# An adaLN transformer block in f32 on one core: the work of the last two batches placed anew, and the last sums turned by TensorE in two parts

## The chip, the cores and the metric

The kernel runs on one core of a Trainium2 chip. Its engines are TensorE (PE, with its weight loads shown as PEld), VectorE (DVE), ScalarE (ACT), GpSimd (POOL) and SyncE (SP), which here issues nearly all transfers. The metric is the time of one execution on the device in microseconds, lower is better; three runs stand beside one profiled execution.

## The reference

Eight batches of 1024 tokens with 256 features, all in f32. A modulation of six vectors per batch (shift, scale and gate, twice) comes from a small product. Then:

```
h = layernorm(x) * (1 + ca) + sa
q, k, v = split(h @ w_in.T)                     # 16 heads of 16
attn = softmax(causal(q k^T / 4)) v
x = x + ga * (attn @ w_out.T + b_out)
h = layernorm(x) * (1 + cb) + sb
prev = h shifted by one token, zero ahead of the first
xr = mu_r * h + (1 - mu_r) * prev ;  xk = mu_k * h + (1 - mu_k) * prev
x = x + gb * sigmoid(xr @ W_r.T) * (relu(xk @ W_k.T)^2 @ W_v.T)
```

The second half needs each token's neighbour, so the second chunk of a batch needs one column ("edge") of the first.

## The kernel before

**Tiling.** A batch b is cut into chunks c of 512 tokens (x is c = 0, y is c = 1 in the tables below). Heads go in groups of four; a unit u = 4b + g is one group of one batch, 32 units in all. Each head sits in a strip of 32 partitions. The scores of a unit are computed twice: `maxima` (S) makes them with the queries on partitions (`pp`), in two banks at a time from the pool `ps_s` (2 buffers of two banks), and DVE takes the largest of each row, adding a causal mask on diagonal blocks; `subtract` turns the maxima (`pmx`) and writes their negative into a spare row of q (`q<-mrow`, a transfer). `weights` (T) makes the scores again with the keys on partitions (`pw`, one bank per head, four banks from the pool `ps_t`, 4 buffers); ACT takes the exponential out of each bank and POOL clears the masked triangle. `attend` multiplies the weights with v, which has a column of ones, so each head's sum comes out as an extra row (`po`, ACT copies it, POOL adds the later parts). The pieces of a unit are the steps a to e (diagonal blocks) and 0 to 3 (whole blocks); the last two units (30 and 31) use the parts f, g, h, i so that chunk 0 is done first.

**The order.** One step of the program (`step`, line 977) takes one piece of T, LAG = 9 places behind S, interleaves the products of both, and then places small work: what `soon` holds for this step, the fill of this step from the tables, and `attend` of the piece before. There are 290 pieces, steps 0 to 298; from step 290 on there is no S left ("alone"). The tables POST, PREP and END name, by step relative to a batch's first, when the parts of `post(b, c)` are placed: load, bias, project0/2 (`py`, attention output times w_out, added to x by DVE), stats and norm (DVE and POOL, on ACT in the ordered stretch), turn (`ptb`, transposes by PE, evacuated by ACT), mix (POOL: difference of neighbours), mixed (DVE: four multiply-adds of 128x512), receptance0/2 (`pr`, tanh on ACT), key0/1 (`pk`, relu on ACT, square on POOL), value0/2 (`pkv`, times r on DVE, added to x on POOL, then the output's transfer). POST for batch 6 starts at step 261; END places x of batch 7 there too, and `tail` does y of batch 7 after the last step.

**What fixes the order.** PE's queue is always in the order of the program text. While `strict` is set (all of the steps), DVE, ACT, POOL and SP keep it too, so an instruction that waits holds up all that stands behind it on its engine. In `tail` a scheduler orders the other engines. `later` puts a transfer off to the next step.

**Sums.** For most units the row of sums goes out and comes back through memory: `gather` stores o (`od`), loads oT from it, and every second unit `spread_sums`, `invert`, `write_over`, `read_over` and `divide` follow over seven steps. For chunk 1 of units 30 and 31, `gather_last` (line 686) does it on the chip: four transposes by PE (`psum`), a reciprocal and a broadcast on DVE (`wide`), a product with the identity (`pinv`), a multiply on DVE, then four transfers of 16 partitions from o into oT.

All small products and turns take their bank from `ps_t` through `bank`, the pool that also holds the four banks of `pw`. After the last step the kernel does x's key and value, and then `tail`.

Of the kernel before, what the change touches and what calls it, by code (L numbers as in the profile page):

```python
# [14 lines left out]
P = 128  # L15
# [57 lines left out]
def adaln_block(  # L73
# [23 lines left out]

    def bank(name):
        return ps_t.tile([P, CW], F32, tag="t", name=name)

    issued = {}
    strict = [False]
# [533 lines left out]
    def groups_of(u):  # L636
        return GROUPS_APART if u >= B * NG - 2 else GROUPS
# [32 lines left out]
    def gather(u, c):  # L670
# [12 lines left out]
            lambda: sync.dma_start(S["oT"][at : at + HG * HD, g // 2, :], od[:, :HD, :])  # L683
        )

    def gather_last(u, c):

        o = U[u]["o", c]
        b, g = divmod(u, NG)
        pt = bank(f"psum{u}")  # L690
        for t in range(NT):
            pe.transpose(pt[:, t * P : (t + 1) * P], o[:, t * P : (t + 1) * P], ident)
        inv = sb.tile([P, NT, HG], F32, tag="few", bufs=2, name=f"inv{u}")
        dve.reciprocal(inv, pt.rearrange("p (t j s) -> p t j s", t=NT, s=ST)[:, :, :, HD])
        wide = sb.tile([P, NT, HG, ST], F32, tag="over", bufs=2, name=f"wide{u}")
        dve.tensor_copy(wide, inv.unsqueeze(3).to_broadcast([P, NT, HG, ST]))
        po = bank(f"pinv{u}")
# [9 lines left out]
        for j in range(HG):  # L707
            at = (g % 2) * HG * HD + j * HD
            queue = act if j % 2 and u == B * NG - 1 else sync
            queue.dma_start(  # L710
                A[b, c]["oT"][at : at + HD, g // 2, :], o[j * ST : j * ST + HD, :]
            )

    def spread_sums(b, c, d):

# [29 lines left out]
    def post(b, c):  # L745
# [12 lines left out]
            return S["x"][:, t0 : t0 + 2, :].rearrange("p t e -> p (t e)")  # L758

        def project(t0):  # L760
            py = bank(f"py{b}_{c}_{t0}")
            rows(py, S["oT"], G[b]["wo"], (t0, t0 + 1))
            dve.tensor_add(flat(t0), flat(t0), py)

# [36 lines left out]
            )  # L801

        def receptance(t0):
            pr = bank(f"pr{b}_{c}_{t0}")
            rows(pr, S["mix"], wr_sb, (t0, t0 + 1))
            r = sb.tile([P, CW], F32, tag="r", bufs=2, name=f"r{b}_{c}_{t0}")
            act.activation(r, pr, AF.Tanh, scale=0.5)
            S["r", t0] = r

        def key(e):  # L810
            pk = bank(f"pk{b}_{c}_{e}")
# [12 lines left out]
            pool.tensor_mul(ka, ka, ka)  # L824

        def value(t0):
            pv = bank(f"pkv{b}_{c}_{t0}")
            rows(pv, S["ka"], G[b]["wv"], (t0, t0 + 1))
            r = S["r", t0]

            dve.scalar_tensor_tensor(r, r, 1.0, pv, ALU.add, ALU.mult)
            pool.tensor_add(flat(t0), flat(t0), r)
            if t0:
                later(lambda: sync.dma_start(tokens(out, b, c), S["x"]))

        def tail():

            def both(f):  # L840
                f(0)
                f(1)
# [2 lines left out]
                return slice(half * CW // 2, (half + 1) * CW // 2)  # L845

            both(lambda half: project(2 * half))
            st = sb.tile([P, NT, 6], F32, tag="st", bufs=2, name="st_last")
            mv = sb.tile([P, NT, 2], F32, tag="mv", bufs=2, name="mv_last")
            rs = sb.tile([P, NT], F32, tag="rs", bufs=2, name="rs_last")  # L850
# [2 lines left out]
            def normal(half):  # L853
                ts = (2 * half, 2 * half + 1)
                for t in ts:
                    dve.bn_stats(st[:, t, :], S["x"][:, t, :])
                    dve.bn_aggr(mv[:, t, :], st[:, t, :])
                of = slice(2 * half, 2 * half + 2)
                dve.tensor_scalar_add(rs[:, of], mv[:, of, 1], EPS)
                pool.tensor_tensor(rs[:, of], rs[:, of], m_half[:, of], ALU.pow)  # L860
                for t in ts:
                    dve.tensor_scalar(
                        h[:, t, :],
                        S["x"][:, t, :],
                        mv[:, t, 0:1],
                        rs[:, t : t + 1],
                        ALU.subtract,
                        ALU.mult,
                    )

            both(normal)
            h2T = sb.tile([P, DC, CW + 1], F32, tag="h2T", name="h2T_last")
            pool.tensor_copy(h2T[:, :, 0:1], A[b, 0]["edge"])
# [95 lines left out]
            value0=lambda: value(0),  # L969
            value2=lambda: value(2),  # L970
            tail=tail,
        )

# [38 lines left out]
    def finish(T, now):  # L1012
# [240 lines left out]
```

## Time and profile before

| | us |
|---|---|
| median of three runs (1415.96 to 1418.1) | 1417.32 |
| the profiled execution, own time | 1422.07 |
| its span, first to last instruction | 1420.3 |
| PE busy | 1392.3 |
| DVE, ACT, POOL busy | 1062.8, 894.0, 553.3 |
| step 290 (first without S), start of its `pw_h` | 1325.2 |
| last `po_i` ends | 1380.5 |
| first `py` of the tail | 1394.05 |
| last product ends | 1415.6 |

The page gives busy times over the span, then the span in 40 slices as tenths, and then groups. In a line of the timeline stand the start, the time, the engine, the line of the program, the operation, out<-in with their shapes, how many instructions were merged, and in brackets the idle time before it with what ended it. In a line of stretches stand the stretch, its length, busy time and number of instructions of PE, PEld, DVE, ACT and POOL, then the granted clock of PE as a share, the DMA share and GB/s. All small operations carry the line of one helper (L115), so they are told apart by the names of their tiles. A name that ends in `_last` belongs to the tail.

### The profile page before, as it was taken

What the parts mean: (1) busy time and instruction counts of PE and PEld (TensorE: products, weight loads), DVE (VectorE), ACT (ScalarE), POOL (GpSimd) and SP (SyncE); (2) the same over time, 40 slices, a digit from 0 to 9 for tenths busy, and PEclk for the clock granted to TensorE, in tenths of its full rate; (3) what the DMA queues carried; (4) which work ended last, traced back from release to release, by engine and by line L of the source; (5) the groups of instructions that cost most, each with busy time, mean ns of one, the idle gap of its engine ahead of it and who ended that gap; (6) DMA issues with size and microseconds to landing.
All of it is one profiled execution on the core that took longest, in us unless ns stands there. A gap on an engine that the chain in (4) does not pass through costs nothing.

```text
span 1420.3 us, 29753 instructions
## 1 busy us (share of the span) xinstructions
PE 1392.3 (98%) x11256; PEld 765.3 (54%) x11256; DVE 1062.8 (75%) x2869; ACT 894.0 (63%) x1693; POOL 553.3 (39%) x840
## 2 busy tenths in 40 slices
PE   9999999999999999999999999999999999999997
PEld 5544555555554555555555555545555555455455
DVE  6777787788777777788777887787777887887234
ACT  3466676666676666666666766766666666575441
POOL 1142242445422444425433454324534344244341
PEclk9999999999999999999999999999999999999988
DMA  5512423232222323231232322223231321201111
GB/s 190 183 34 81 128 76 113 62 102 84 91 73 69 107 83 110 68 101 64 83 113 62 106 80 98 66 69 106 84 105 59 106 89 38 83 32 43 41 32 33
DMA packets 81271, 118.96 MB, mean 84 GB/s; under 512 B 10208, under 2 KB 38752, under 8 KB 81128
## 3 DMA queue, kind: packets, MB, share of 16 engines
q1 hardware_dynamic: 80792, 116.74, 25.4%
q8 instruction: 88, 1.44, 0.4%
q14 instruction: 55, 0.45, 0.1%
q10 hardware_dynamic: 336, 0.33, 0.1%
HBM read 71.17 MB, written 45.09 MB: 82 GB/s over the span
## 4 chain that ended last, share of the span: by engine, by line
PE 91%; DMA 3%; DVE 2%; ACT 2%; POOL 1%; issue 1%; SPq 0%; POOLq 0%; ACTq 0%; DVEq 0%
PE pw L115 12%; PE po L115 8%; PE pp L115 7%; PE pq L115 6%; PE po_c L115 5%; PE po_e L115 5%; PE py L115 4%; PE pkv L115 4%; PE pr L115 4%; PE pk L115 4%; PE pv L115 4%; PE pw_a L115 3%; PE pw_e L115 2%; PE pmx L115 2%; PE pw_c L115 2%; PE pp_d L115 2%
## 5 line engine op out<-in xcount | busy, mean ns | idle before, releaser
L115 DVE TENSOR_REDUCE max<-pp 128x2 f32<-128x1024 f32 x256 | 301.9, 1218 | 63.4 <-PE pp L115 61.2
L115 ACT ACTIVATE w<-pw 128x512 f32<-128x512 f32 x512 | 265.2, 602 | 95.3 <-PE pp L115 59.6
L115 PE MATMUL pw<-q,k 32*128 32x512 f32 x1024 | 267.0, 618 | 0.4 <-ACT w_i L115 0.4
L115 PE MATMUL pp<-k,q 32*128 32x512 f32 x1024 | 256.7, 620 | 0.0
L115 PEld LDWEIGHTS pw<-q,k 32*128 32x128 f32 x1024 | 108.7, 184 | 99.8 <-issue 57.4
L115 DVE DVE_READ_ACCUMULATOR2_ANT max<- 128x1 f32 x1024 | 144.8, 141 | 0.0
L115 DVE CUSTOM_DVE_ANT_0 pp_c<-pp_c,mask 128x256 f32<-128x256 f32 x240 | 102.3, 436 | 46.8 <-PE pp_c L115 40.6
L115 DVE CUSTOM_DVE_ANT_0 pp_b<-pp_b,mask 128x128 f32<-128x128 f32 x240 | 102.3, 437 | 43.5 <-PE pp_b L115 37.2
L115 DVE CUSTOM_DVE_ANT_0 pp_e<-pp_e,mask 128x512 f32<-128x512 f32 x128 | 88.3, 707 | 52.5 <-PE pp_e L115 50.3
L115 DVE CUSTOM_DVE_ANT_0 pp_d<-pp_d,mask 128x128 f32<-128x128 f32 x240 | 102.4, 437 | 28.9 <-PE pp_d L115 22.8
L115 PE MATMUL po<-w,v 128*32 128x512 f32 x1024 | 123.1, 598 | 0.0
L115 PE MATMUL pq<-hT,wqk_sb 128*128 128x512 f32 x240 | 114.3, 608 | 1.0 <-ACT hT L115 1.0
L115 POOL TENSOR_TENSOR xb<-xb,r 128x512 f32<-128x512 f32 x30 | 41.4, 1379 | 148.9 <-DVE r L115 123.9
L115 DVE CUSTOM_DVE_ANT_0 pp_a<-pp_a,mask 128x512 f32<-128x512 f32 x128 | 87.8, 707 | 12.9 <-PE pp_a L115 10.8
L115 ACT ACTIVATE w_a<-pw_a 128x512 f32<-128x512 f32 x128 | 66.2, 602 | 41.8 <-PE pp_a L115 40.3
L115 POOL TENSOR_TENSOR rsb<-rsb,m_half 128x2 f32<-128x2 f32 x30 | 21.5, 715 | 177.5 <-DVE rsb L115 177.4
L115 POOL TENSOR_TENSOR o<-o,more 128x512 f32<-128x512 f32 x62 | 79.1, 1276 | 28.2 <-ACT more L115 28.2
L115 PEld LDWEIGHTS pp<-k,q 32*128 32x128 f32 x1024 | 82.7, 183 | 3.9 <-DVE max L115 3.6
L115 ACT ACTIVATE w_d<-pw_d 128x512 f32<-128x512 f32 x120 | 63.1, 601 | 19.9 <-PE pp_e L115 19.6
L115 ACT ACTIVATE w_e<-pw_e 128x512 f32<-128x512 f32 x128 | 66.2, 603 | 14.2 <-PE pp_c L115 13.4
L115 ACT ACTIVATE w_b<-pw_b 128x512 f32<-128x512 f32 x120 | 62.1, 602 | 18.1 <-PE pp L115 17.6
L115 ACT ACTIVATE w_c<-pw_c 128x512 f32<-128x512 f32 x120 | 62.2, 603 | 14.9 <-PE pp_b L115 10.7
(207 smaller groups left out, 3046.4 us busy)
## 6 DMA issues: line engine op xcount, KB each, us to landing
od<-o SPq DMA_DIRECT2D x62, 256.0 KB
pad<-qk SPq DMA_DIRECT2D x60, 256.0 KB
q<-pad SPq DMA_DIRECT2D x30, 512.0 KB
k<-pad SPq DMA_DIRECT2D x30, 512.0 KB
xa<-in_x SPq DMA_DIRECT2D x16, 512.0 KB
xb<-in_x SPq DMA_DIRECT2D x16, 512.0 KB
oT<-od SPq DMA_DIRECT2D x62, 128.0 KB
ov<-over SPq DMA_DIRECT2D x31, 256.0 KB
```

What stands on the lines that cost most here:

```text
L115: made = f(*args, **kwargs)
```

## The change

- A flag `late` is set at the first step without S. From then on `bank_apart` takes the banks of `py`, `pr`, `pk` and `pkv` from the pool of the maxima (`ps_s`).
- `gather_last` is cut in two: `turn_sums` (psum, reciprocal, wide) one step after a unit's end, and the rest (pinv, multiply, transfers) one step later. Units 30 and 31 now do this for chunk 0 too, which went through memory before; its four transfers are put off by a step.
- A table POST_LAST takes the place of POST for batch 6 while batch 7 is attended, and END names earlier steps for x of batch 7.
- A step without S and without fill gets five transposes of the identity (`heat`); this is the case in step 298.
- x's key of batch 7 goes around the last `pinv`; x's value is cut into its product (`multiplied`) and the rest (`valued`), which `tail` places between its own parts. The second half of the tail's normalisation goes from DVE to ACT.

```diff
+    late = [False]
+    def bank_apart(name):
+        if late[0]:
+            return ps_s.tile([P, 2, CW], F32, tag="s", name=name)[:, 0, :]
+        return bank(name)
...
-    def gather_last(u, c):
+    def turn_sums(u, c):
         o = U[u]["o", c]
-        pt = bank(f"psum{u}")
+        pt = bank(f"psum{u}_{c}")
         for t in range(NT):
             pe.transpose(pt[:, t * P : (t + 1) * P], o[:, t * P : (t + 1) * P], ident)
...
+        U[u]["wide", c] = wide
+    def gather_last(u, c):
+        o, wide = U[u]["o", c], U[u]["wide", c]
...
+        def side_by_side():
+            for j in range(HG):
+                at = (g % 2) * HG * HD + j * HD
+                queue = act if j % 2 and c and u == B * NG - 1 else sync
+                queue.dma_start(
+                    A[b, c]["oT"][at : at + HD, g // 2, :], o[j * ST : j * ST + HD, :]
+                )
+        if c:
+            side_by_side()
+        else:
+            later(side_by_side)
...
-        def value(t0):
-            pv = bank(f"pkv{b}_{c}_{t0}")
+        def multiplied(t0):
+            S["pv", t0] = pv = bank_apart(f"pkv{b}_{c}_{t0}")
             rows(pv, S["ka"], G[b]["wv"], (t0, t0 + 1))
-            r = S["r", t0]
+        def valued(t0):
+            r, pv = S["r", t0], S["pv", t0]
...
             both(lambda half: project(2 * half))
+            other["multiplied0"]()
...
+                if half:
+                    pool.tensor_mul(away, mv[:, of, 0], rs[:, of])
+                    pool.tensor_scalar_mul(away, away, -1.0)
+                for n, t in enumerate(ts):
+                    if half:
+                        act.activation(h[:, t, :], S["x"][:, t, :], AF.Identity,
+                            bias=away[:, n : n + 1], scale=rs[:, t : t + 1])
+                        continue
...
-            both(turned)
+            turned(0)
+            other["multiplied2"]()
+            turned(1)
...
             both(mixed_half)
+            other["valued0"](), other["valued2"]()
...
         alone = not (T and S)
+        if not S and not late[0]:
+            late[0] = True
...
+        if not S and not fill:
+            pt = bank_apart(f"heat{now}")
+            for n in range(5):
+                pe.transpose(pt[:, :P], ident, ident)
...
-            if u >= B * NG - 2 and c:
-                soon.append((now + 1, lambda: gather_last(u, c)))
+            if u >= B * NG - 2:
+                soon.append((now + 1, lambda: turn_sums(u, c)))
+                soon.append((now + 2, lambda: gather_last(u, c)))
                 return
...
+    POST_LAST = """
+    -12 x.load; -6 x.bias; 4 x.project0; 6 x.project2; 7 x.stats0; 7 y.load; 8 x.stats1; 8 y.bias;
+    9 x.norm0; 9 y.project0; 10 x.norm1; 10 x.turn; 11 x.mix; 11 y.project2; 12 x.mixed00;
+    12 y.stats0; 13 x.mixed01; 13 x.mixed10; 13 x.receptance0; 14 x.mixed11; 15 x.receptance2;
+    15 y.stats1; 16 y.norm0; 17 x.key0; 17 y.norm1; 18 x.key1; 18 y.turn; 19 y.mix; 20 x.value0;
+    20 y.mixed00; 21 y.mixed01; 21 y.mixed10; 22 x.value2; 22 y.mixed11; 22 y.receptance0;
+    23 y.receptance2; 24 y.key0; 25 y.key1; 26 y.value0; 27 y.value2
+    """
...
     END = """
-    26 x.load; 28 x.bias; 32 x.project0; 32 x.project2; 33 x.stats0; 33 x.stats1; 34 x.norm0;
-    34 x.norm1; 35 x.turn; 35 x.mix; 36 x.mixed00; 36 x.mixed01; 36 x.mixed10; 36 x.mixed11;
-    36 y.load; 37 y.bias; 37 x.receptance0; 37 x.receptance2
+    16 x.load; 18 x.bias; 26 y.load; 28 x.project0; 28 y.bias; 29 x.project2; 30 x.stats0;
+    30 x.stats1; 31 x.norm0; 32 x.norm1; 32 x.turn; 33 x.mix; 34 x.mixed00; 34 x.mixed01;
+    34 x.mixed10; 34 x.mixed11; 35 x.receptance0; 36 x.receptance2
     """
...
-            place(POST, at, x=ready[b - 1][0], y=ready[b - 1][1])
+            place(POST if b < B - 1 else POST_LAST, at, x=ready[b - 1][0], y=ready[b - 1][1])
...
+    for n, f in ((1, "key0"), (2, "key1")):
+        soon.append((len(slots) + n, ready[B - 1][0][f]))
+    soon.sort(key=lambda z: z[0])
...
-    for f in ("key0", "key1", "value0", "value2"):
-        ready[B - 1][0][f]()
-    ready[B - 1][1]["tail"]()
+    ready[B - 1][1]["tail"](ready[B - 1][0])
```

For comparison, the entries of POST that y used before: project0 15, project2 17, turn 20, mix 21, mixed 22 to 25, receptance 28 and 29, key 29 and 31, value 33 and 35.

More of the change, by code (lines that the diff above doesn't have):

```diff
@@ L684, in gather @@
         )
-    def gather_last(u, c):
+    def turn_sums(u, c):
         o = U[u]["o", c]
-        b, g = divmod(u, NG)
-        pt = bank(f"psum{u}")
+        pt = bank(f"psum{u}_{c}")
         for t in range(NT):
             pe.transpose(pt[:, t * P : (t + 1) * P], o[:, t * P : (t + 1) * P], ident)
-        inv = sb.tile([P, NT, HG], F32, tag="few", bufs=2, name=f"inv{u}")
+        inv = sb.tile([P, NT, HG], F32, tag="few", bufs=2, name=f"inv{u}_{c}")
         dve.reciprocal(inv, pt.rearrange("p (t j s) -> p t j s", t=NT, s=ST)[:, :, :, HD])
-        wide = sb.tile([P, NT, HG, ST], F32, tag="over", bufs=2, name=f"wide{u}")
+        wide = sb.tile([P, NT, HG, ST], F32, tag="over", bufs=2, name=f"wide{u}_{c}")
         dve.tensor_copy(wide, inv.unsqueeze(3).to_broadcast([P, NT, HG, ST]))
-        po = bank(f"pinv{u}")
+        U[u]["wide", c] = wide
+    def gather_last(u, c):
+        o, wide = U[u]["o", c], U[u]["wide", c]
+        b, g = divmod(u, NG)
+        po = bank(f"pinv{u}_{c}")
         for t in range(NT):
@@ L706, in gather_last @@
         dve.tensor_mul(o, o, po)
[L707 to L712, printed above, removed]
+        def side_by_side():
[9 more added lines that the diff above has]
+            later(side_by_side)
     def spread_sums(b, c, d):
@@ L760, in project @@
         def project(t0):
-            py = bank(f"py{b}_{c}_{t0}")
+            py = bank_apart(f"py{b}_{c}_{t0}")
             rows(py, S["oT"], G[b]["wo"], (t0, t0 + 1))
@@ L803, in receptance @@
         def receptance(t0):
-            pr = bank(f"pr{b}_{c}_{t0}")
+            pr = bank_apart(f"pr{b}_{c}_{t0}")
             rows(pr, S["mix"], wr_sb, (t0, t0 + 1))
@@ L810, in key @@
         def key(e):
-            pk = bank(f"pk{b}_{c}_{e}")
+            pk = bank_apart(f"pk{b}_{c}_{e}")
             for d in range(DC):
@@ L834, in value, with tail @@
                 later(lambda: sync.dma_start(tokens(out, b, c), S["x"]))
-        def tail():
+        def tail(other):
             def both(f):
@@ L860, in normal @@
                 pool.tensor_tensor(rs[:, of], rs[:, of], m_half[:, of], ALU.pow)
-                for t in ts:
+                if half:
[3 more added lines that the diff above has]
+                    if half:
+                        act.activation(
+                            h[:, t, :],
+                            S["x"][:, t, :],
+                            AF.Identity,
+                            bias=away[:, n : n + 1],
+                            scale=rs[:, t : t + 1],
+                        )
+                        continue
                     dve.tensor_scalar(
@@ L869, in normal @@
                     )
+            away = sb.tile([P, 2], F32, tag="away", bufs=2, name="away_last")
             both(normal)
@@ L968, in post @@
             key1=lambda: key(1),
-            value0=lambda: value(0),
-            value2=lambda: value(2),
+            multiplied0=lambda: multiplied(0),
+            multiplied2=lambda: multiplied(2),
+            valued0=lambda: valued(0),
+            valued2=lambda: valued(2),
+            value0=lambda: (multiplied(0), valued(0)),
+            value2=lambda: (multiplied(2), valued(2)),
             tail=tail,
```

## The prediction

> **What bounds the kernel now.** I read the page's busy shares first, then its slices, then the stretches of the last 130 us by the granted clock, then the timeline of TensorE (PE) with the waits in brackets, and last the other engines around those waits. Over the span PE is the bound, and the clock it was granted sags only in the last two slices:
>
> ```profile
> PE 1392.3 (98%) x11256; PEld 765.3 (54%) x11256; DVE 1062.8 (75%) x2869; ACT 894.0 (63%) x1693; POOL 553.3 (39%) x840
> PEclk9999999999999999999999999999999999999988
> ```
>
> These are stretches of the last 130 us; the third last column is the granted clock, 0.50 in each:
>
> ```profile
> 1335.30:1338.70 3.40, 3.40 (x8) 0.90 (x11) 0.00 (x0) 0.84 (x3) 0.63 (x1) 0.51 0.00 0
> 1362.70:1366.10 3.40, 3.40 (x10) 2.65 (x9) 0.08 (x1) 1.09 (x3) 0.83 (x2) 0.50 0.00 0
> 1372.90:1376.30 3.40, 3.40 (x9) 2.69 (x10) 1.04 (x2) 0.96 (x3) 2.22 (x5) 0.50 0.01 4
> 1400.30:1407.00 6.70, 5.04 (x14) 3.90 (x15) 5.58 (x16) 2.11 (x5) 0.70 (x1) 0.50 0.00 0
> ```
>
> The waits of PE there, and the one of DVE from which the first of them comes:
>
> ```profile
> 1297.01 2.33 DVE L115 SCALAR_TENSOR_TENSOR mix<-step,mus,h2T 128x512 f32<-128x512 f32 x2 [1.19 <-POOL step L115]
> 1300.59 1.07 PE L115 MATMUL pp_i<-k,q 32*128 32x256 f32 x8 [1.75 <-DVE max L115]
> 1362.38 3.53 PE L115 MATMUL pkv<-wvb,ka 128*128 128x256 f32 x8 [1.31 <-ACT w_e L115]
> 1381.33 0.66 PE L115 MATMUL psum<-ident,o 128*128 128x128 f32 x4 [0.87 <-DVE o L115]
> 1382.89 1.81 PE L115 MATMUL pinv<-ident,wide 128*128 128x128 f32 x8 [0.90 <-DVE wide L115]
> 1390.93 3.29 PE L115 MATMUL pkv<-wvb,ka 128*128 128x256 f32 x14 [1.02 <-POOL ka L115]
> 1394.05 3.62 PE L115 MATMUL py<-wob,oT 128*128 128x256 f32 x16
> 1399.33 0.78 PE L115 MATMUL pt_last<-ident,h_last 128*128 128x128 f32 x4 [1.66 <-DVE h_last L115]
> 1401.96 1.14 PE L115 MATMUL pt_last<-ident,h_last 128*128 128x128 f32 x4 [1.85 <-DVE h_last L115]
> 1403.01 3.75 PE L115 MATMUL pr<-wr_sb,mix_last 128*128 128x256 f32 x8
> 1408.53 1.89 PE L115 MATMUL pr<-wr_sb,mix_last 128*128 128x256 f32 x8
> ```
>
> A busy PE is not a fast one: the same `pr` takes 3.75 us at 1403 and 1.89 at 1408. In the last 130 us the clock falls at 1301.2, 1335.3, 1345.6, 1362.7, 1372.9, 1383.1 and 1400.3; all gaps are multiples of 3.41 us, and each fall lasts 3.4 us (the last twice that). So the clock is decided on a grid of 3.41 us, and a stretch costs 1.7 us where PE has work throughout. Ahead of each fall stand either a gap of PE or the 32-row products `pw` without `pp` beside them: 0.44 us of gap was enough at 1372.3.
>
> Prices at full clock: a product of eight 128x256 records (py, pr, pk, pkv) 1.73 us (1408.53 to 1410.25); pw with pp 1.86; pw alone 1.9; po 1.86, po_i 2.36; a final sum's four transposes 0.66; pinv 0.9 (half of the 1.81 at half clock).
>
> **The change part by part.** Steps count from 0; all up to 289 have maxima (S) beside weights (T); steps 290 to 298 have weights alone. In the profile 290 begins at 1325.2, and po_i ends at 1380.5.
>
> *Steps 265 to 289 (batch 6 sooner; chunk 0's last sums on chip).* Six products (one pr, two pk, two pkv of batch 6, one py of batch 7) leave the alone steps for these: 6 x 1.73 = 10.4 us, work that PE does either way, so zero. Added on PE: psum and pinv for two units, 2 x 1.56 = 3.1, 2.8 as their drains overlap (bounds 2.4 and 3.6, at half clock partly). SP loses two stores through memory, their reads, and one chain of inverses; it gains eight issues on oT at 0.62 (2.47 for four). Four of those stand in step 288 ahead of the last batch's out and of `q<-mrow`, which is wanted four steps later; py of step 289 wants them. The multiply is done about 4 us into 287, issues and landing take 2.5 + 2.0 (a store of od at 1308.93, its read at 1310.94), py starts 12 us into it: hidden, with 3.3 us to spare. Without it PE would wait for the remainder.
>
> DVE is the danger here. In steps 280 to 282 the masked maxima stand close: e 3.0, h 2.5 + r 0.69 + mix 0.70, i 3.35 + reciprocal 0.53 + two mixes 1.4 + join 0.1: 12.3 us against PE's 2.3 + 3.35 + 4.2 = 9.9. DVE begins a step 1 us behind PE and PE may run two banks ahead, so I take 1.6 us of gaps (bounds 0, the lead covers it, and 5: the excess plus two waits for POOL like the 1.19 above). Steps 271 to 276 come out even (DVE: maxima 15.3, four mixes 2.8, two statistics 2.5, an addition 0.7, a reciprocal 0.5: 21.8; PE: six times 1.86, ptb 0.9, three products 5.2, pmx 0.4, two po of a first half 4.7: 22.4), so I take 0.4. In return the gap at 1298.8 (1.75), its half clock (1.7) and 0.35 before it go: y's mixes come a step after POOL's subtraction and beside r, not into h. One half stretch after the new gaps, one in two: 0.85. Sum: +3.8 - 2.85 - 2.8 = **-1.85** (loss).
>
> *Steps 290 to 298.* Lost before: gaps 0.44 + 0.29 + 0.96 + 1.31 + 0.44, pw slower for its banks 0.4 (2.27) and 0.7 (pw_e 2.59), four half stretches 6.8: 11.3. Late products now sit in the banks of maxima, so pr no longer queues behind exponentials, and the 0.96 of pinv goes because pw of the next step lies between it and psum. What stays: pw of step 292 after pw_i (0.44 + 0.4), psum behind POOL's addition (0.3), pw_e right behind pw_3 (0.7). What is new: the turn of batch 7's mix (ptb) now stands in 293, ahead of pw_2, behind four exponentials (2.07) and two halves of hb (0.52 each) on ACT; it is ready about 1.85 us after pw_1, psum fills 0.75: 1.1 us (bounds 0 and 1.9), and all later weights queue behind it. That is 2.9. Half clock: less full-width work lies between the pw, so I take three chances of 3/4 at 1.7: 3.8 (bounds 0 and 6.8). Heat, five transposes: 0.5 (bounds 0.4 and 1.1, by the same count at half clock). Sum: 11.3 - 6.7 - 0.5 = **+4.1**.
>
> The Trainium skill ("TensorE: Matmul & The Clock Gate", HAM oscillation) says that only idle gaps of more than about 3.4 us cost the clock. The row of 0.44 us above differs, so the measurement decides; by the rule the half-clock terms of this sum would be zero. The same page (Part 4, PE-mode transpose) says that transposes do not count as activity for the clock; no run here shows it, and it speaks against heat: the 0.5 would buy nothing, and psum with ptb would leave a cold window for certain.
>
> *The tail, from po_i's end (t).* Before: psum at t + 0.87, py at t + 13.6, end at t + 39.8. After, s = t + 0.87: psum to s + 0.45, pk to 2.2, pinv to 3.05 (wide waits inside pk), multiply 3.25 to 3.95. The issues on SP and ACT take 1.15 and 1.42, the second leaves about 0.7 in, landing 2.0: oT at s + 6.7. The second pk ends at 4.8, so PE waits 1.95: a new stall, which was covered by pkv before. py starts at t + 7.6, **6.0 sooner**. From py (p): the first turn at p + 5.3 as before, pkv now in the wait ahead of it; second pkv to p + 7.7. The second turn gets later: on DVE a valued r (0.69) stands ahead of rs_last, on POOL an addition to xb (1.27) stands ahead of its power (0.70), then away 0.20 + 0.23, two hb on ACT 1.04: p + 10.6 instead of 7.9. pr of the first half queues behind that turn on PE, from 11.1 instead of 9.0. At full clock from there (1.73 each for pr, pk, pr, pk, pkv, pkv) the end is p + 26.45, before 26.25 with two half stretches. Half clock after the new 1.95 (6 in 10) and the new 3.1 (7 in 10) at 1.7: 2.2. Gain: 6.0 - 0.2 - 2.2 = **+3.6** (bounds 5.8 without half clock, -1.4 with both and DVE's mixes stretched by POOL as at 1297, 1.17 for 0.70, over eight short ones).
>
> Sum: -1.85 + 4.1 + 3.6 = 5.9 us. The profiled execution took 1422.07 (span 1420.3 and 1.8 around it), 4.75 over the median of runs; I take the difference off the median: 1417.32 - 5.9 = **1411.4**.
>
> **The rivals.**
> - Slower, by DVE: the mixes and maxima stall behind POOL in the shared steps, as at 1297. One such stall cost 1.75 + 1.7 = 3.45. The other terms leave 8.7 us over (3.8 + 4.1 + 3.6 - 2.8); from three stalls they are gone, and with four the time is 1417.32 + 5.1 = 1422.4. For: 12.3 against 9.9. Against: one stall in 25 steps before, and two mixes at 1257 without any wait.
> - The alone steps gain nothing: four half stretches and gaps as before, 11.3 again. -1.85 - 0.5 + 3.6 = 1.2: 1416.1. For: pw and ptb leave PE narrow. Against: three of the five waits before were for banks or for pinv.
> - The tail does not do what it says, because the second turn is later and everything behind it stands at half clock: tail 0, total 2.3: 1415.0. For: POOL's addition ahead of the power. Against: py's 6.0.
> - No half clock after the change in the alone steps and the tail: 3.8 + 2.2 + 0.85 more: 12.7, 1404.6. For: fewer gaps. Against: seven falls in 130 us.
>
> **How the numbers follow.** A measurement of this kernel tells about 0.2% (2.8 us) from no change. Chances: forecast 0.50, DVE 0.09, alone steps 0.16, tail 0.12, full clock 0.13. The range takes in the full-clock side to 1405.5 and the two weak gains to 1416.8; beyond lie most of the DVE case and the rest of full clock, 2 in 10. Faster: forecast 0.47, full clock 0.13, tail 0.06, alone 0.06: 0.72. Slower: DVE and 0.01: 0.10. Same: 0.18.
>
> **What would show it.** No gap of 1.75 for pp_i, but gaps `<-DVE max` or at pmx in steps 281 to 283; pr and pk without `<-ACT w` ahead; ptb waiting for ACT hb; from po_i's end to py 7.6 us with `<-DMA oT` of 2; from the first to the second pt_last 5.3; the end 36 us after po_i; six half stretches or fewer from 1290 on. Wrong it would be if DVE waits for POOL repeatedly, if the oT of step 289 lands late, or if the earlier places of batch 6 stop PE before step 277.

## The result, and the profile after

Over 16 runs of each kernel, the median goes from 1418.44 us (1415.92 to 1423.62) to 1409.74 us (1406.92 to 1415.51). The ratio is 0.9941, with a 95% interval of 0.9928 to 0.9954: **0.59% or 8.4 us faster**, and the interval excludes no change. The prediction was 1411.4 with a gain of 5.9 us and a range from 1405.5 to 1416.8. The profiled execution of the changed kernel took 1412.37 us (span 1410.7), against 1422.07 (1420.3) before.

From the page, the lines of busy time and of the granted clock in 40 slices:

```profile
PE 1382.5 (98%) x11285; PEld 758.2 (54%) x11285; DVE 1063.3 (75%) x2872; ACT 894.7 (63%) x1695; POOL 550.9 (39%) x841
PEclk9999999999999999999999999999999999999999
```

PE has 29 more instructions (24 of chunk 0's sums, 5 of the heat) and is busy for 9.8 us less. That can't be work that was saved; it is work that ran at a higher clock, and the two slices with an 8 are gone. The stretches at half clock that are left in the last 190 us (stretch, its length, busy times and counts of PE, PEld, DVE, ACT, POOL, then the granted clock):

```profile
1351.90:1358.70 6.80, 6.80 (x27) 2.47 (x25) 3.04 (x5) 1.98 (x4) 1.95 (x2) 0.50 0.04 10
1392.90:1396.30 3.40, 3.30 (x10) 2.59 (x11) 1.56 (x5) 1.54 (x4) 1.44 (x1) 0.51 0.30 102
```

That makes three stretches of 3.41 us where before had eight (the last fall before was twice as long). The waits of PE from the timeline of the changed kernel, with what ended each in brackets:

```profile
1246.02 0.33 PE L123 MATMUL ptb<-ident,hb 128*128 128x128 f32 x1 [1.51 <-ACT hb L123]
1260.79 1.56 PE L123 MATMUL pr<-wr_sb,mix 128*128 128x256 f32 x6 [1.73 <-DVE mix L123]
1300.64 0.60 PE L123 MATMUL pmx<-ident,max 128*4 128x128 f32 x4 [0.31 <-DVE max L123]
1341.06 2.27 PE L123 MATMUL pw<-q,k 32*128 32x512 f32 x8 [0.62 <-ACT w_i L123]
1349.31 0.33 PE L123 MATMUL ptb<-ident,hb 128*128 128x128 f32 x1 [0.75 <-ACT hb L123]
1375.66 0.66 PE L123 MATMUL psum<-ident,o 128*128 128x128 f32 x4 [0.84 <-DVE o L123]
1382.79 3.26 PE L123 MATMUL py<-wob,oT 128*128 128x256 f32 x14 [1.72 <-DMA oT<-o]
1387.62 0.81 PE L123 MATMUL pt_last<-ident,h_last 128*128 128x128 f32 x4
1392.98 1.40 PE L123 MATMUL pt_last<-ident,h_last 128*128 128x128 f32 x4 [2.83 <-ACT h_last L123]
1394.17 2.92 PE L123 MATMUL pr<-wr_sb,mix_last 128*128 128x256 f32 x8
1398.66 1.89 PE L123 MATMUL pr<-wr_sb,mix_last 128*128 128x256 f32 x8
```

The gap of 1.75 us for `pp_i` is gone, `pr` and `pkv` no longer wait for exponentials, and `pinv` no longer waits. In their place stand two gaps in the shared steps, at 1246 and 1260, that were not there before, one ahead of `ptb` in step 293, and in the tail 1.72 for oT and 2.83 for the second turn.

To see where the time went I cut every trace at three marks. The first (the "anchor" of two expectations below) is the start of the last row of `po_c` that lies ahead of everything changed; then come the start of step 290 (`pw_h`), the end of the last `po_i`, and the end of the span. "Full clock" takes half of PE's busy time in each half-clock stretch off, as far as the stretch lies in these parts; it is an estimate. The end of the span is taken to one decimal, so the tails are good to 0.05 us.

| us | before | after | gain | at full clock, before | after |
|---|---|---|---|---|---|
| shared steps, first mark to step 290 | 108.63 | 120.51 | -11.88 | | |
| alone steps | 55.27 | 39.17 | 16.10 | | |
| both together | 163.90 | 159.68 | 4.22 | 155.4 | 156.3 |
| tail | 39.84 | 35.89 | 3.95 | 35.6 | 34.2 |

Six products moved from the alone into the shared steps, so only the third row can be read without pricing them. The sum is 8.2 us; another 1.4 of the difference of the two spans lies ahead of the first mark, where nothing was changed; the profile before has a stretch at half clock there (1212.5 to 1215.9), the one after has none. At full clock the changed kernel takes 0.9 us *more* for the steps than the old one and 1.4 less for the tail. **The rest of the gain, 7.7 us, is half clock that does not happen**: 8.5 to 3.4 us lost in the steps, 4.2 to 1.65 in the tail.

These are one profile of each kernel, but the runs say the same. Each run has its span and its mean granted clock on record, and the clock is 0.50 or 1.00 in all traces here; so the share missing from 1.00, times the span, is an estimate of what the run lost to half clock (good to 0.7 us, since the clock has three digits, and high where PE had no work in a stretch). The 16 runs of the changed kernel lost 1.4 to 9.9 us, 5.2 in the mean; 63 runs of the kernel before, taken beside the experiments on three chips, lost 14.2 in the mean (13.8 to 14.7 by chip). Without these losses the mean spans are 1403.5 and 1403.8 us: at full clock the two kernels are equally fast.

### The profile page after: what moved, and what is told of

Read it like the earlier page. It is cut to its first block, busy times and chain, and to the rows that moved or that the text cites. A ratio compares the mean times of both kernels' runs of the same rounds, so it can differ in the third digit from the quotient of the medians.

```text
span 1410.7 us, 29817 instructions
## 1 busy us (share of the span) xinstructions
PE 1382.5 (98%) x11285; PEld 758.2 (54%) x11285; DVE 1063.3 (75%) x2872; ACT 894.7 (63%) x1695; POOL 550.9 (39%) x841
## 4 chain that ended last, share of the span: by engine, by line
PE 91%; DVE 4%; DMA 2%; ACT 2%; POOL 1%; issue 1%; ACTq 0%; SPq 0%; DVEq 0%; POOLq 0%
PE pw L123 12%; PE po L123 8%; PE pp L123 7%; PE pq L123 7%; PE po_c L123 5%; PE po_e L123 5%; PE pr L123 4%; PE py L123 4%; PE pv L123 4%; PE pkv L123 4%; PE pk L123 4%; PE pw_a L123 3%; PE pw_e L123 3%; PE pw_c L123 2%; PE pmx L123 2%; PE pw_b L123 2%
## 5 line engine op out<-in xcount | busy, mean ns | idle before, releaser
L123 DVE CUSTOM_DVE_ANT_0 pp_a<-pp_a,mask 128x512 f32<-128x512 f32 x128 | 87.8, 707 | 12.6 <-PE pp_a L123 10.4
```

What stands on the lines that cost most here:

```text
L123: made = f(*args, **kwargs)
```

## The experiments

Every kernel below is the changed kernel with the edit shown. "Ratio" is against the kernel before, with its 95% interval; the changed kernel has 0.9941 [0.9928, 0.9954]. Intervals of this width separate two such kernels from about 3 us on, so smaller effects are read from the traces, one profile of each.

The split of the spans by the clock, as above, for all runs of each kernel (means):

| kernel | runs | lost to half clock, us | span without it, us |
|---|---|---|---|
| before | 63 | 14.2 | 1403.8 |
| changed | 16 | 5.2 | 1403.5 |
| tables as before | 9 | 7.7 | 1401.7 |
| banks as before | 9 | 6.7 | 1404.0 |
| tables and banks as before | 12 | 9.7 | 1404.3 |
| no heat | 6 | 5.6 | 1403.1 |
| tail's order as before | 12 | 7.4 | 1404.5 |
| sums in one part | 12 | 10.0 | 1407.8 |
| turn a step later | 6 | 6.3 | 1401.0 |
| POOL in order in the tail | 12 | 6.6 | 1402.7 |
| keys behind `pinv` | 6 | 6.6 | 1402.8 |
| the better parts | 6 | 8.0 | 1399.8 |

The runs of one kernel differ by several us in the third column and by little more than one in the last. Against the changed kernel, differences of less than about 1 us in the last column, or of less than 2 to 3 in the third, are not clear of that spread.

### The places of the tables

The tables POST (also for batch 6) and END as before; all else as changed.

```diff
-            place(POST if b < B - 1 else POST_LAST, at, ...)
+            place(POST, at, ...)
     END = """
-    16 x.load; 18 x.bias; 26 y.load; 28 x.project0; ...
+    26 x.load; 28 x.bias; 32 x.project0; 32 x.project2; ...
```

> Both tables of places as before the change (POST for batch 6, END for x of batch 7); the banks, the two-part sums, heat and the tail stay as changed. Theory 'places': the 5.7 us that the alone steps gained come mostly from here, since six products leave the steps in which only narrow weights keep PE busy and the half-clock stretches come back; 4 to 6 us slower than the changed kernel, about 1414.5, with three or four half-clock stretches after step 290 instead of one double one. Rival 'banks and tail': places only move the same work and bring 4 us of new gaps of their own (ptb 1.5, pr 1.7), so 1409 to 1411, no difference.

Measured: 1410.61 us, ratio 0.9935 [0.9913, 0.9958]. So the theory that the earlier places carry the gain of the alone steps falls. In the trace, without them the shared steps take 112.88 us, the alone steps 45.21, together 158.09 against 159.68 with them, and the alone steps have no stretch at half clock at all. The `pp_i` gap is back, with its own fall:

```profile
1297.50 0.92 PE L123 MATMUL pp_i<-k,q 32*128 32x256 f32 x8 [1.03 <-DVE max L123]
```

```profile
1299.40:1306.30 6.90, 6.90 (x26) 3.81 (x28) 4.42 (x18) 1.17 (x2) 0.64 (x1) 0.51 0.35 97
1306.50:1404.00 97.50, 87.52 (x537) 53.06 (x525) 41.04 (x73) 42.67 (x83) 36.87 (x51) 1.00 0.11 32
```

The first fence is from the timeline, the second shows stretches of the same trace: a double one at half clock soon after the gap, and then full clock to the last product. Over its nine runs this kernel loses 7.7 us to half clock against 5.2 with the new places, and is 1.8 us shorter without that loss: as far as nine runs tell, the new places buy about as much half clock as their gaps and moves cost.

### The banks

The late products take `ps_t` again; only the heat keeps the other pool.

```diff
-        if late[0]:
+        if late[0] and name.startswith('heat'):
```

> Late py, pr, pk and pkv take the banks of the weights again; all else as changed. Theory 'banks count': py of step 290, the two pr and pk queue behind exponentials again, 0.4 to 1.3 us each, plus at most one half-clock stretch more: 1.5 to 3.5 us slower than the changed kernel. Rival 'places made it idle': few products are left in the alone steps, so it is within 1 us of the changed kernel.

Measured: 1413.18 us, ratio 0.9944 [0.9925, 0.9964]. In the trace the alone steps take 37.11 us, where the kernel without heat (below), which has the banks and equally no stretch at half clock there, takes 35.92. The banks are worth 1.2 us with the new tables, too little for the time to show.

### The tables and the banks together

Both undone at once, with the on-chip sums, the heat and the new tail kept.

```diff
-        if late[0]:
+        if late[0] and name.startswith('heat'):
...
-            place(POST if b < B - 1 else POST_LAST, at, ...)
+            place(POST, at, ...)
     END = """
-    16 x.load; 18 x.bias; 26 y.load; 28 x.project0; ...
+    26 x.load; 28 x.bias; 32 x.project0; 32 x.project2; ...
```

> Both tables as before and late products in the banks of the weights, as before; the two-part sums of both chunks, heat (which falls into step 291 here) and the tail stay as changed. Theory 'either is enough': the clock falls of the alone steps go away when their products no longer wait for exponentials, be it by other banks or by having left; with neither, two to four half-clock stretches come back after step 290 and the time is 3 to 7 us over the changed kernel (1413 to 1417). Rival 'the sums did it': the falls came from the gap between psum and pinv alone, so they stay away and the time is within 1.5 us of the changed kernel.

Measured: 1415.29 us, ratio 0.9972 [0.9953, 0.9990]. This one loses 4.4 us of the 8.4 by the ratios, and 4.5 us more to half clock than the changed kernel over its runs. Its alone steps take 50.70 us with two falls, each at the end of a wait that the kernel before had too:

```profile
1361.37 3.66 PE L123 MATMUL pkv<-wvb,ka 128*128 128x256 f32 x8 [1.30 <-ACT w_e L123]
1371.74 5.32 PE L123 MATMUL pr<-wr_sb,mix 128*128 128x256 f32 x16 [0.43 <-ACT w_i L123]
```

```profile
1361.40:1364.80 3.40, 3.40 (x8) 2.70 (x9) 0.00 (x0) 1.38 (x3) 0.83 (x2) 0.50 0.00 0
1371.60:1375.00 3.40, 3.26 (x8) 2.64 (x9) 1.46 (x2) 1.23 (x4) 2.06 (x6) 0.50 0.09 27
```

A product that waits for a bank behind exponentials is what both parts remove, the tables by moving it away and the banks by giving it another bank. Either is enough; the second adds little. That is why neither showed much when undone alone.

### The heat

```diff
-        if not S and not fill:
+        if False:
```

The five transposes, whose result nothing reads, are left out.

> Without the five transposes of heat (0.77 us on PE in step 298). Theory 'heat buys nothing': the last po_i waits for POOL's mask of w_i anyway, so the end of po_i and the time stay, within 1 us. Rival 'heat holds the clock': the stretch of 3.41 us after it falls to half, 1 to 1.7 us slower, seen as clock 0.5 between po_i and py.

Measured: 1411.11 us, ratio 0.9932 [0.9907, 0.9958]. Without them the first product of `po_i` waits instead, and the alone steps take 35.92 us. In the kernel of the next section, which has the heat and full clock there too, they take 35.90.

```profile
1368.40 1.07 PE L123 MATMUL po_i<-w_e,v 128*32 128x512 f32 x8 [0.71 <-ACT w_i L123]
```

The heat fills 0.7 us in which PE had nothing to do. It costs nothing, and no run shows that it buys anything.

### The tail's order

x's value is done before the tail, as in the kernel before; the parts inside the tail go.

```diff
-            other["multiplied0"]()
...
-            other["multiplied2"]()
...
-            other["valued0"](), other["valued2"]()
...
+    for f in ("value0", "value2"):
+        ready[B - 1][0][f]()
```

> x's two value products and their additions go ahead of the tail in one piece, as before the change; all else as changed. Theory 'py early, second turn late': py starts about 3 us later after po_i (10.9 instead of 8.0), but the second turn comes 2.5 us sooner after the first (2.7 instead of 5.4) since POOL's addition no longer stands ahead of its power; in sum 0.5 to 2 us slower. Rival 'the interleaving is the gain': the tail loses its whole 4 us, 1413.5.

Measured: 1412.84 us, ratio 0.9952 [0.9935, 0.9970]. Its tail takes 37.81 us, 1.9 more than the changed kernel's 35.89, with one fall in each:

```profile
1381.20 3.29 PE L123 MATMUL pkv<-wvb,ka 128*128 128x256 f32 x14 [1.84 <-POOL ka L123]
1384.33 3.62 PE L123 MATMUL py<-wob,oT 128*128 128x256 f32 x16
1389.45 0.87 PE L123 MATMUL pt_last<-ident,h_last 128*128 128x128 f32 x4 [1.51 <-DVE h_last L123]
1393.07 0.33 PE L123 MATMUL pt_last<-ident,h_last 128*128 128x128 f32 x1 [2.75 <-ACT h_last L123]
```

PE waits 1.84 us for the square on POOL and 1.51 for the first turn; `py` starts 11.24 us after the last `po_i`, where in the changed kernel two of its records run at 5.67 and the rest from 7.98 on. The second turn comes 3.6 us after the first instead of 5.36, so 1.7 of the 3.3 go back there. This is the trade that the prediction described.

### The sums in one part

The rest of the final sums (`pinv`, multiply, transfers) goes into the same step as their turn, for all but the last unit's chunk 1.

```diff
-                soon.append((now + 2, lambda: gather_last(u, c)))
+                soon.append((now + (2 if c and u == B*NG-1 else 1), lambda: gather_last(u, c)))
```

> pinv and the rest follow psum in the same step for the first three of the four sums (the very last stays in two parts). Theory 'two parts hide the reciprocal': each of the three pinv waits 0.9 us for wide, 2.9 us in sum, and in the alone steps the gap brings a half-clock stretch now and then: 2 to 5 us slower than the changed kernel. Rival: in the steps with maxima another product could not have run anyway, since DVE is as full as PE; less than 1 us.

Measured: 1419.06 us, ratio 0.9996 [0.9982, 1.0011]. The whole gain is gone, 7.8 us by the ratios, where I had expected 2 to 5. The waits, from PE's timeline:

```profile
1305.86 2.05 PE L123 MATMUL pinv<-ident,wide 128*128 128x128 f32 x8 [3.79 <-DVE wide L123]
1327.54 1.24 PE L123 MATMUL pinv<-ident,wide 128*128 128x128 f32 x8 [1.80 <-DVE wide L123]
```

And what DVE did ahead of the first of them, from its timeline:

```profile
1294.13 2.77 DVE L123 SCALAR_TENSOR_TENSOR mix<-step,mus,h2T 128x512 f32<-128x512 f32 x1
...
1304.38 0.70 DVE L123 CUSTOM_DVE_ANT_0 pp_e<-pp_e,mask 128x512 f32<-128x512 f32 x1
1305.00 0.14 DVE L123 DVE_READ_ACCUMULATOR2_ANT max<- 128x1 f32 x1
1305.00 0.25 DVE L123 RECIPROCAL inv<-psum 128x16 f32<-128x16 f32 x1
1305.28 0.43 DVE L123 COPY wide<-inv 128x512 f32<-128x512 f32 x1
```

The reciprocal and its broadcast take 0.7 us. They stand in DVE's order behind two mixes, a join and four masked maxima, and DVE has no pause from 1293.53 on (the mix of 2.77 us at 1294.13 is part of that); `pinv` waits for all of that, and everything on PE waits behind `pinv`. The clock is at half from 1304.5 to 1311.4 and from 1328.4 to 1331.9. Over the runs this kernel loses 4.8 us more to half clock than the changed one and is 4.3 longer without that. The second step is not there to hide 0.7 us of arithmetic but DVE's queue.

### The two new gaps in the shared steps

Only POST_LAST is changed: x's turn and mix and its first `mixed` and receptance come one step later.

```diff
-    9 x.norm0; 9 y.project0; 10 x.norm1; 10 x.turn; 11 x.mix; 11 y.project2; 12 x.mixed00;
-    12 y.stats0; 13 x.mixed01; 13 x.mixed10; 13 x.receptance0; 14 x.mixed11; 15 x.receptance2;
+    9 x.norm0; 9 y.project0; 10 x.norm1; 11 x.turn; 11 y.project2; 12 x.mix;
+    12 y.stats0; 13 x.mixed00; 13 x.mixed01; 14 x.mixed10; 14 x.receptance0; 15 x.mixed11; 15 x.receptance2;
```

> In the new table x.turn, x.mix, x.mixed of batch 6 and receptance0 come one step later each. Theory: the two gaps that the changed kernel has in the steps with maxima (ptb behind ACT's hb 1.51 and 0.16, pr behind DVE's mix 1.73) go, since each stands in the same step as what it waits for; from the anchor to step 290 it takes 117 instead of 120.5 us, 2 to 3.4 us faster than the changed kernel, about 1407. Rival: DVE is as full as PE there, so the wait moves to pp behind the maxima; no difference.

Measured: 1409.33 us, ratio 0.9927 [0.9904, 0.9949]. In the trace both gaps go. The turn waits 0.32, the receptance nothing, and the shared steps take 117.64 us instead of 120.51:

```profile
1248.12 1.14 PE L123 MATMUL ptb<-ident,hb 128*128 128x128 f32 x8 [0.32 <-ACT w_c L123]
...
1260.56 1.99 PE L123 MATMUL pr<-wr_sb,mix 128*128 128x256 f32 x8
```

So these 2.9 us were the price of placing the second half of the norm and the turn in one step, and the mixes and the receptance that reads them too close together; the earlier places as such did not need it. The ratios (0.14% apart) could not tell this; without the half clock, the six runs are 2.5 us shorter than the changed kernel's in the mean.

### The order on POOL in the tail

POOL keeps the program's order in the tail, and the copy of the edge is made ahead.

```diff
+            h2T = sb.tile([P, DC, CW + 1], F32, tag="h2T", name="h2T_last")
+            pool.tensor_copy(h2T[:, :, 0:1], A[b, 0]["edge"])
+            pool.always = True
             both(lambda half: project(2 * half))
```

> In the tail POOL keeps the order of the program text, so both powers and the two small products come before the additions of x's value to xb (the copy of the edge is made first). Theory: the second turn is late because of POOL's addition (1.45 us) and DVE's stretched rs_last; it comes 3.5 to 4.2 us after the first instead of 5.4, the half-clock stretch after it gets shorter or goes, 1 to 2.5 us faster. Rival: DVE's r and the two halves of the normalisation on ACT set it; 0.5 us or less.

Measured: 1410.60 us, ratio 0.9941 [0.9924, 0.9959], the same time as the changed kernel. The second turn comes 4.36 us after the first instead of 5.36, and the tail takes 35.16 us instead of 35.89. This is how POOL and DVE stood in the changed kernel:

```profile
1389.22 1.45 POOL L123 TENSOR_TENSOR xb<-xb,r 128x512 f32<-128x512 f32 x1 [2.17 <-DVE r L123]
1390.78 0.87 POOL L123 TENSOR_TENSOR rs_last<-rs_last,m_half 128x2 f32<-128x2 f32 x1
```

```profile
1389.47 1.23 DVE L123 TENSOR_SCALAR rs_last<-mv_last 128x2 f32<-128x2 f32 x1
```

The addition to `xb` does stand ahead of the power, as the prediction had it. It also holds up DVE's `rs_last`, which feeds that power: 1.23 us beside it, 0.17 for the same operation of the first half, and 0.16 in this kernel, where the addition comes later:

```profile
1388.27 0.16 DVE L123 TENSOR_SCALAR rs_last<-mv_last 128x2 f32<-128x2 f32 x1
```

Out of its way the turn gains the 1.0 us; the rest of the tail takes 0.3 of it back. Both are less than I had expected (a turn after 3.5 to 4.2 us, 1 to 2.5 us in all), and the stretch at half clock behind the turn stays (1391.7 to 1395.1).

### The keys of the last chunk

Both halves of x's key go behind the last `pinv`'s place, none ahead of it.

```diff
-    for n, f in ((1, "key0"), (2, "key1")):
+    for n, f in ((2, "key0"), (2, "key1")):
```

> Both key products of x come after the last pinv instead of one before it. Theory 'the multiply is what py waits for': pinv starts 0.9 us sooner (it waits for wide 0.9 instead of standing behind a product of 1.73), oT lands as much sooner and the second wait shrinks: py 6.9 to 7.3 instead of 8.0 us after po_i, 0.7 to 1.1 us faster, if no half-clock stretch comes of the gap ahead of pinv; with one it is 0.6 slower. Rival: as now, within 0.3 us.

Measured: 1412.31 us, ratio 0.9941 [0.9918, 0.9964]. `pinv` waits 0.90 us and the clock falls behind it; `py` starts at 8.50 us after `po_i` instead of 7.98, without a wait of its own for oT, and the tail takes 37.04 us.

```profile
1376.66 1.19 PE L123 MATMUL pinv<-ident,wide 128*128 128x128 f32 x8 [0.90 <-DVE wide L123]
```

```profile
1377.60:1381.00 3.40, 3.40 (x6) 1.40 (x5) 0.69 (x1) 0.00 (x0) 0.00 (x0) 0.50 0.18 37
```

With a stretch at half clock behind the gap the expectation had `py` 0.6 us later; it is 0.5, and the tail 1.2 longer. Whether the stretch comes in each execution isn't known: over the runs this kernel loses 1.4 us more to half clock than the changed one and is 0.7 shorter without it, neither clear of the spread, and the times are the same.

### Do transposes keep the clock?

In place of the five transposes of step 298 come 80 of them in one kernel, and 40 ordinary products of the same size (80 records) in the other.

```diff
-            for n in range(5):
+            for n in range(80):
```

```diff
-            for n in range(5):
-                pe.transpose(pt[:, :P], ident, ident)
+            for n in range(40):
+                pe.matmul(pt[:, :P], ident, ident, start=True, stop=True)
```

> 80 transposes of the identity in step 298 instead of five, about 8.6 us at full clock with PE never idle. Theory 'turns count as work': the granted clock stays at 1.00 through the stretch. Rival 'they do not': it falls to 0.50 at the end of the first 3.41 us that lies within them, each transpose then takes 0.21 instead of 0.107 us, and the stretch takes 11 to 14 us.

> The control: 40 products of the identity with itself, two records of 128 columns each, so as many records in as much time, in the same place. Both theories: the clock stays at 1.00 and the stretch takes about 8.6 us.

The 80 transposes took 8.95 us, the 80 records of products 9.20, one profile of each. The stretch of the transposes, from the trace of the first, and that of the products, from the second:

```profile
1374.80:1383.70 8.90, 8.90 (x88) 8.73 (x88) 0.00 (x0) 1.64 (x4) 1.28 (x2) 1.00 0.00 1
```

```profile
1372.20:1381.30 9.10, 9.10 (x87) 8.98 (x83) 0.00 (x0) 1.64 (x4) 1.29 (x2) 1.00 0.00 1
```

The clock stays at 1.00 in both, for more than two of the grid's windows. The Trainium skill ("TensorE: Matmul & The Clock Gate", Part 4, PE-mode transpose) says that transposes don't count as busy for the clock; for f32 transposes these rows differ. The trace lists the transposes as MATMUL, like the products; whether the mode that the page means was on, it does not tell.

### The better parts together

The step later for x's turn, POOL's order in the tail, and the normalisation of batch 7 in the alone steps on DVE instead of ACT.

```diff
-            if strict[0]:
+            if strict[0] and not late[0]:
                 act.activation(
```

> The changed kernel with batch 6's turn, mix and receptance0 a step later (as in the run before), the normalisation of batch 7's x on DVE in the alone steps, and POOL in the order of the text in the tail. Theory: the gaps ahead of ptb in step 293 (0.75 and 0.15) go, from the anchor to step 290 117.6 us instead of 120.5, alone steps 35 at full clock, tail 35.2 or less; 3 to 6 us faster than the changed kernel: 1404 to 1407, with the spread that the half-clock stretches leave. Rival: DVE's bigger load or a new wait eats it; 1409 or more.

Measured: 1407.36 us, ratio 0.9922 [0.9898, 0.9947]: the fastest median of all kernels here, 11.1 us below the kernel before. Its advantage over the changed kernel is within the intervals, and by the ratios it is 2.7 us, a little under the 3 to 6 expected. In the trace the first two parts do what they did alone: shared steps 117.64, tail 35.18; the alone steps take 35.97 at full clock. Over the runs it is the shortest without half clock (1399.8), but loses 8.0 us to it. The third does not pay, since the second half of `hb` now stands behind the reciprocal and its broadcast:

```profile
1347.99 1.09 PE L123 MATMUL ptb<-ident,hb 128*128 128x128 f32 x6 [0.91 <-DVE hb L123]
```

The wait was 0.75 + 0.15 with ACT.

## Why the prediction was right, and where its steps were not

The direction, the total (8.4 against 5.9) and all three terms came out with the right sign. With the moved work at the prediction's 10.4 us, the shared steps lost 1.5 (predicted 1.85), the alone steps gained 5.7 (4.1) and the tail 3.95 (3.6).

**Shared steps.** The term came out close, but by errors that offset each other. Right: the `pp_i` gap of 1.75 and its half clock went. The transfers of the new sums stayed hidden: no `py` of the shared steps waits for oT. Wrong in place: the 1.6 us of DVE gaps in steps 280 to 283 came as 0.31 at one `pmx` and 0.15 at one `pp_e`, near the lower bound of that term, where DVE's lead covers its excess. The 0.4 us in steps 271 to 276 came as 1.67 for ACT's `hb` and 1.73 for DVE's mix. The prediction had added up DVE's load there and found it even with PE's. What failed is that step: a sum over six steps says nothing of two operations that depend on each other and stand in the same step. Moving them one step gave 2.9 us back. New gaps came to 4.2 us in all (0.32 of them at another `pmx`), against 2.0 predicted. For half clock behind them 0.85 had been allowed, one chance in two. None came in this profile; in three of the nine traces with these places (keys, transposes, products) a fall follows the turn's wait of 1.5 us.

The sums of chunk 0 cost more than the 2.8 predicted: without gaps and half clock, the shared steps take 104.8 us in the kernel before and 108.2 in the one with neither tables nor banks, which differ there by these sums, 3.4 us. What offset the gaps and these sums is the price of the moved work, which the prediction put at 1.73 us for each product wherever it stands, 10.4 in all. The kernel with neither tables nor banks and the one with the moved turn differ in the shared steps by the six products, and have the same gaps in all (1.39 and 1.26 us) and no half clock: 109.57 and 117.64 us. So six products cost 8.1 us there, 1.35 each, though each takes 1.7 to 1.9 from start to start. The weights and maxima around them take less in return: the 16 records of `pw_f` and `pp_e` take 2.70 us to the next start at 1278.78 in the first of these traces, 1.84 at 1282.86 in the second. That they fill time in which PE waits for DVE's maxima is likely, but not shown.

**Alone steps.** Two stretches at half clock against 2.25 predicted, the wait at the turn 0.90 against 1.1, psum 0.23 against 0.3. The 0.5 for the heat was wrong: it lies inside a wait of 0.7 for ACT, so it costs nothing. The reason given for the gain was right in kind, the end of queueing for banks behind exponentials, but the prediction counted on both the move and the banks; either alone does it. The first two rivals didn't come. The last, no half clock at all, nearly came in 3 of the 16 runs (a granted clock of 0.999), at 1406.9 to 1407.3 us against its 1404.6. The one that put DVE's stalls in the shared steps had its mechanism, though: with the sums in one part, `pinv` stalls 3.79 and 1.80 and the gain is gone. The prediction took the cut in two parts at its cost on PE and never priced what it prevents.

**Tail.** The step-by-step chain held: first `py` that needs oT at 7.98 us after `po_i` (7.6 predicted), its wait 1.72 (1.95), the turns 5.36 apart (5.3), the end at 35.9 (36), one stretch at half clock (1.3). The rival in which the tail gives all back did not come; what it named, POOL's addition ahead of the power, costs 1.0 at the turn.

**Half clock.** The three terms add up to 2.3 us more than predicted. Of these, 1.25 are half clock in the steps: 5.1 us regained, 3.85 predicted (6.8 - 3.8, and 1.7 - 0.85). Another 0.7 are the steps at full clock: 0.9 lost, 1.6 predicted (2.7 in the shared steps, less 1.1 in the alone ones). How much half clock one execution meets differs from run to run. The falls of one trace lie on a grid: 1351.88 and 1392.84 in the changed kernel are twelve times 3.413 apart, 1377.59 and 1394.66 in the kernel with the keys moved are five times. The same products behind the same 0.9 us wait at `ptb` met a fall in three traces (changed, the moved turn, POOL's order) and none in six (banks, no heat, the tail's order, the keys, the transposes, the products). A stretch costs 1.7 us, and the runs of the changed kernel spread over 8.6. That half clock makes this spread is shown by the clocks: spans of 1405.1 to 1413.8 us lie within 1401.6 to 1404.3 without it. That the place of the program on the grid decides which falls come is argued, not shown: from the start of that `ptb` to the next point of the grid it is 2.57 us in the changed kernel and with POOL's order, and 0.60 with the moved turn, where falls came, and 2.67 without heat, where none did.

The rule that the prediction had set against its rows, that PE must not idle for more than about 3.4 us (the Trainium skill, "TensorE: Matmul & The Clock Gate", HAM oscillation; that only such gaps cost the clock was the prediction's reading), is not enough here: falls stood at or behind waits of 0.43 and 0.90 us. Another section of the same page (A second HAM failure mode: psum-queue depth-cycling) tells of a kernel whose frequent short idle times between groups of products made the clock oscillate, and the rows are of that kind.

**Open.** The kernel with neither tables nor banks has two stretches in the alone steps, the one before has four; which of the on-chip sums, the second step for `pinv` and the heat took the other two wasn't tried one by one. The stretches by place are counted in one profile of each kernel, and why one execution meets a fall at a wait and another does not stays open.

## What to carry to other kernels

Where an engine keeps a written order, cost a move by the pair of operations that depend on each other in one step and by all that stands ahead of them in the slowest queue, not by the load summed over several steps. Price the moved work by what the whole stretch gains in length: six products of 1.73 us cost 8.1 us beside the maxima. When two parts of a change remove the same wait, undoing each alone shows little; undo both. Where falls of the clock stand behind short waits, such waits can cost more than their length: here 5 of 8 stretches at half clock went in the profiles, 9.0 us in the mean of the runs, and without half clock the two kernels differ by less than 1 us.

## What the runs showed of the hardware that was not expected

- f32 transposes hold the clock as products do: 80 of them in 8.95 us at 1.00, 0.11 us each.
- The clock can fall at a wait of 0.43 us in the alone steps. In the shared steps, where `pp` stands beside `pw`, it fell behind the 1.75 us at `pp_i` (before), behind the 1.51 at the turn in three of nine traces, and behind the 1.73 at `pr` in none of nine.
- A small DVE operation beside an addition on POOL can be stretched: `rs_last` from 0.17 to 1.23 us, a mix of 128x512 from 0.65 to 2.77 beside masks and an addition. Not every one is: `step_last` of 128x256 beside the same addition took 0.40 us (1389.15 in the changed kernel).
